# A bidirectional state-space layer with a soft mixture of experts: a PSUM bank held one step longer and one more step before each norm is scaled

## The chip, the cores and the metric

The kernel runs on one core of one Trainium2 chip. The metric is the device time of one execution in microseconds (us); of several executions the median is given. Shorter is better. The five engines of the core run at the same time, each with its own queue: PE (TensorE) multiplies and transposes, DVE (VectorE), ACT (ScalarE) and POOL (GpSimd) work on 128 partitions by so many columns, and SP (SyncE) starts DMAs, as ACT's queue does here as well.

## The reference, cut to what matters

The input is 16 batches of 512 positions by 256 channels, float32. One layer of two parts is computed, each with a residual and a layer norm after it:

```python
xf, res = jnp.split(x @ in_proj_w.T, [512], axis=-1)
xf = silu(causal_dw_conv(xf, conv_w, conv_b))            # 4 taps along the positions
y  = ssm(xf, res, forward weights)
xb = silu(causal_dw_conv(xf, conv_b_w, conv_b_b))        # the backward taps read xf
y  = (y + ssm(xb, res, backward weights, reverse=True)) @ out_proj_w.T
x  = layernorm(x + y)                                    # the "m" norm
x  = layernorm(x + soft_moe(x))                          # the "c" norm
```

`ssm` makes a step size `dt` by a softplus, then for each of 512 channels and 16 states a recurrence along the 512 positions, multiplies it by a factor of its own and sums over the states; `res` gates the sum. The mixture has 16 experts of 64 slots: after a norm, softmax weights gather positions into slots (dispatch), each expert is a gated pair of matrices, and a second softmax brings the slots back to positions (combine).

## The kernel before, in words

`seq_layers` runs over the 16 batches. Each batch has four calls of `scan_part`, for forward and backward (r = 0, 1) and for two pairs of channel chunks (p = 0, 1), in the order (0,0), (1,0), (0,1), (1,1). A call runs over the 16 states in pairs and over two chunks of 128 channels: 16 half-steps. A batch has 64 of them and the kernel 1024.

**A half-step** makes two states of one chunk, each of 128 x 512. POOL multiplies `db` = `du` x `bs` (L403), ACT makes the decay by an exp (L420) and the factor `th` by a tanh (L422), DVE runs the recurrence as a scan (L426 forward, L428 backward) and `hg` = (`th` + 1) x `h` (L431), POOL multiplies `hg` by `cs` (L432), and PE adds `hg` by eight transposing matmuls into the PSUM accumulators `acc` (L347), two half-steps later. `bs` and `cs` come by DMA from SP's queue. For the pairs with the states 5 and 13 (`DIAG`) one state of the pair is made on PE by a diagonal matrix (`hd`, L381). Buffers: `db` 3, `hg` 4, `th` 3, `h` 3 in PSUM.

**Beside the scan** run generators in three lanes, each an object of the class `Side` (L448 to L510). `prep` makes what the next scans need: `prep_forward` (transposes, projection, forward taps), `turn_back` (the backward taps, L223 to L230), `prep_backward` (silu at L235 and the projection `px`), `prep_pair` (`dt`, `rr`, `du`), `prep_gate` and `turn_pair` (`duT`, copied at L331). `front` holds `finish` (transposes of the gated sum at L598, out projection, residual, norm m) and the dispatch; `back` holds the experts and `combine` (norm c). After each half-step `beside_scan` (L517) calls `take_up` of every lane, then begins pieces of work: one of `prep` each time, one of `front` or `back` when its credit has grown to 1.

**What the marks mean.** A generator stops at a `yield`. A positive number tells how many PSUM banks the next piece needs; `HOLD` says that a bank was filled and that what reads it is to be issued at the next `take_up`; `WAIT` is the same without a bank. There are three banks in a ring (`BANKS`, handed out by `bank` at L105). A piece is not begun if the banks handed out since the oldest one held, and those it needs, are more than three (L486 to L488). A half-step that is about to make a state by the diagonal calls `take_up` once more ahead of it (L440, L441), so a lane that stands at a mark is moved twice in that half-step.

**The order of the work** on each engine is made by a scheduler when the program is built; instructions wrapped in `late` keep their place in program order and the others may be moved ahead.

**The norms.** `row_moments` makes means and variances on DVE. `factors` makes from them the scale and shift on POOL, four operations on 128 x 4 (L575 to L578: `m_rs`, `m_sh`, or `c_rs`, `c_sh`); `finish` makes a second factor `r2` by four more (L624 to L627). `scaled` applies them by four ACTIVATEs of ACT (L583). In `finish` one `WAIT` stands between moments and factors and two between factors and `scaled` (after L627), then come the store of x1 on ACT's queue (L631) and `xn` (L635). In `combine` it is the same (`WAIT`s at L955, L957 and L958); there `put` scales and stores the output on ACT's queue (L930). After the last batch a tail (L997 to L1021) finishes batch 15 and runs the experts and combines of the last two batches, with eight banks; there `combine` scales row by row, without those marks.

**The backward taps.** `taps` makes a convolution of one chunk: an ACTIVATE writes the bank `pb` (L171), DVE adds three taps (L177), the last of which writes to `xb` in SBUF. Its first three columns are complete in the bank only, and ACT copies them (L229).

Of the kernel before, what the change touches and what calls it, by code (L numbers as in the profile page):

```python
# [28 lines left out]
KW = 4  # L29
# [10 lines left out]
HOLD, WAIT, GAP = -1, -2, 8  # L40
# [13 lines left out]
def seq_layers(tc, ident, neghalf, a, out):  # L54
# [20 lines left out]
    nc = tc.nc  # L75
    nb = a["x"].shape[0]
    with ExitStack() as ctx:
# [27 lines left out]
        def bank(name):  # L105
            count[0] += 1
            if tail and count[0] % 8 >= 3:
                return tail[0].tile([P, 512], F32, tag="tps", name=name)
            return ps.tile([P, 512], F32, tag="mps", name=name)
# [54 lines left out]
        def late(ins):  # L164

            return tc.keep_in_program_order(ins)

        def taps(dst, src, w, c, last):

            late(  # L170
                nc.scalar.activation(  # L171
                    dst, src, AF.Identity, bias=w["cb"][:, c : c + 1], scale=w["cw"][:, c, KW - 1 : KW]
                )
            )
            for j in range(1, KW):
                o = last if j == KW - 1 else dst
                ins = nc.vector.scalar_tensor_tensor(  # L177
                    o[:, j:], src[:, : L - j], w["cw"][:, c, KW - 1 - j : KW - j], dst[:, j:], ALU.mult, ALU.add
                )
                if j == 1:  # L180
                    late(ins)
# [41 lines left out]
        def turn_back(b, fwd, out):  # L223
            xb = p1.tile([P, ND, L], F32, tag="xb", name=f"xb_{b}")
            for c in range(ND):
                yield 1
                pb = bank(f"pb_{b}_{c}")
                taps(pb, fwd["u"][:, c, :], side[1], c, xb[:, c, :])
                nc.scalar.copy(xb[:, c, 0 : KW - 1], pb[:, 0 : KW - 1])  # L229
            out["u"] = xb  # L230

        def prep_backward(b, out):
# [348 lines left out]
        def scaled(dst, src, sh, rs):  # L581
            for i in range(src.shape[1]):
                ins = nc.scalar.activation(  # L583
                    dst[:, i, :], src[:, i, :], AF.Identity, bias=sh[:, i : i + 1], scale=rs[:, i : i + 1]
                )
                if i == 0:
                    late(ins)

        def finish(b, y):

            xt = load_x(b)
            for h in range(NL // 2):
                yts = []
                for lc in (2 * h, 2 * h + 1):
                    yield 1
                    pt = bank(f"pyt_{b}_{lc}")
                    for c in range(ND):
                        nc.tensor.transpose(  # L598
                            pt[:, c * P : (c + 1) * P], y[:, c, lc * P : (lc + 1) * P], ident
                        )  # L600
                    yield HOLD
                    yt = p2.tile([P, L], F32, tag="fr", name=f"yt_{b}_{lc}")
                    late(nc.scalar.copy(yt, pt))  # L603
                    yts.append(yt)
                yield GAP + 1
                po = bank(f"po_{b}_{h}")
                for i, yt in enumerate(yts):
                    for c in range(ND):
                        nc.tensor.matmul(  # L609
                            po[:, i * DM : (i + 1) * DM],  # L610
                            yt[:, c * P : (c + 1) * P],
                            outT[:, c, :],
                            start=(c == 0),
                            stop=(c == ND - 1),
                        )
                yield HOLD
                x2 = xt[:, 2 * h : 2 * h + 2, :].rearrange("p c d -> p (c d)")
                late(nc.vector.tensor_tensor(x2, x2, po, ALU.add))
            mv = row_moments(nc, p2, xt, "m1")
            yield WAIT  # L620
            rs, sh = factors(mv, "m1")

            r2 = p2.tile([P, NL], F32, tag="m1_r2", name=f"m1_r2_{b}")
            nc.gpsimd.tensor_tensor(r2, mv[:, :, 1], rs, ALU.mult)  # L624
            nc.gpsimd.tensor_tensor(r2, r2, rs, ALU.mult)
            nc.gpsimd.tensor_scalar(r2, r2, EPS, None, ALU.add)
            nc.gpsimd.tensor_tensor(r2, r2, neghalf[:, :NL], ALU.pow)  # L627
            yield WAIT
            yield WAIT
            scaled(xt, xt, sh, rs)  # L630
            nc.scalar.dma_start(x1_dram[b].rearrange("(c p) d -> p c d", p=P), xt)  # L631
            yield 0
            xn = p1.tile([P, NL, DM], F32, tag="xn", name=f"xn_{b}")
            for i in range(NL):
                ins = nc.scalar.activation(xn[:, i, :], xt[:, i, :], AF.Identity, scale=r2[:, i : i + 1])  # L635
                if i == 0:
                    late(ins)
            yield WAIT
            x2T = p1.tile([P, NM, L], F32, tag="x2T", name=f"x2T_{b}")
            for k in range(NM):  # L640
                yield GAP + 1
                pt = bank(f"px2_{b}_{k}")
                for lc in range(NL):
                    nc.tensor.transpose(
                        pt[:, lc * P : (lc + 1) * P], xn[:, lc, k * P : (k + 1) * P], ident
                    )
                yield HOLD
                late(
                    nc.scalar.activation(
                        x2T[:, k, :], pt, AF.Identity, bias=shift[:, k : k + 1], scale=gain[:, k : k + 1]  # L650
                    )
                )
            nc.scalar.dma_start(x2_dram[b].rearrange("k p l -> p k l"), x2T)
            yield from dispatch(b, xn, x2T)
# [249 lines left out]
        def combine(b, kept=None):  # L904

            own = e_dram[:, b * SL : (b + 1) * SL, :].rearrange("(c j) s o -> j s c o", j=2)
            eos = []
            for c0 in range(0, NSC, 4):
                if wide:
                    t = wide[0].tile([P, 4, DM], F32, tag="ceo", name=f"ceo_{b}_{c0}", bufs=4)  # L910
                else:
                    t = p2.tile([P, 4 * DM], F32, tag="W", name=f"ceo_{b}_{c0}", bufs=3)
                    t = t.rearrange("p (c o) -> p c o", c=4)
                for j in range(2):
                    nc.sync.dma_start(t[j * SL : (j + 1) * SL, :, :], own[j][:, c0 : c0 + 4, :])
                eos.append(t)
            if wide and b % 2:
                x1 = p1.tile([P, NL, DM], F32, tag="x", name=f"cx1_{b}")
            else:
                x1 = p1.tile([P, NL, DM], F32, tag="cx1", name=f"cx1_{b}")  # L920
            nc.sync.dma_start(x1, x1_dram[b].rearrange("(c p) d -> p c d", p=P))
            x2 = [] if kept else [load_x2(b, 0)]
            yield 0

            def moments(lo, hi):
                return row_moments(nc, p2, x1[:, lo:hi, :], f"c{hi - lo}"), f"c{hi - lo}"

            def put(lo, hi, rs, sh):
                scaled(x1[:, lo:hi, :], x1[:, lo:hi, :], sh, rs)
                nc.scalar.dma_start(out[b].rearrange("(c p) d -> p c d", p=P)[:, lo:hi, :], x1[:, lo:hi, :])  # L930

            for lc in range(NL):
                i = f"{b}_{lc}"
                cts, sm = kept.pop((b, lc)) if kept else (yield from weights(b, lc, x2, False))
                yield GAP + 1
                po = bank(f"cpo_{i}")
                for sc in range(NSC):
                    nc.tensor.matmul(  # L938
                        po[:, :DM],
                        cts[sc // 4][:, sc % 4 * P : (sc % 4 + 1) * P],  # L940
                        eos[sc // 4][:, sc % 4, :],
                        start=(sc == 0),
                        stop=(sc == NSC - 1),
                    )
                yield HOLD
                late(
                    nc.vector.scalar_tensor_tensor(
                        x1[:, lc, :], po[:, :DM], sm, x1[:, lc, :], ALU.mult, ALU.add
                    )
                )  # L950
                if kept is not None:
                    put(lc, lc + 1, *factors(*moments(lc, lc + 1)))
            if kept is None:
                stats = moments(0, NL)
                yield WAIT  # L955
                both = factors(*stats)
                yield WAIT  # L957
                yield WAIT  # L958
                put(0, NL, *both)

        FINISH, COMBINE, PAIR = 32, 14, 4
# [106 lines left out]
```

## Time and profile before

| | |
|---|---|
| median of 3 runs | 5432.52 us (5432.14 to 5433.58) |
| profiled execution | 5434.84 us |
| its span in the profile | 5432.9 us |
| mean granted TensorE clock | 0.89 |
| PE busy | 4336.3 us (80%) |
| DVE busy | 4552.0 us (84%) |
| ACT busy | 4091.6 us (75%) |
| POOL busy | 4732.3 us (87%) |
| DMA moved | 907.73 MB, mean 167 GB/s |

The profile is of one execution. The span is from the first recorded instruction to the end of the last; the time of the execution is 1.9 us more. A line of a group names line, engine, operation, output and inputs, and gives after the bar the busy time in us, the mean of one in ns, the idle time just before them and what ended most of it. A line of the waits names the waiting instruction, what it waited for, the total in us, the number of times and the longest. A line of a timeline gives start, duration, engine, line and operation, and in brackets the idle time ahead of it and the instruction that ended it. Idle time on an engine that does not bound a stage costs nothing.

Cut by the end of each batch's last product on POOL, the span falls into batches of these lengths:

| stretch | us |
|---|---|
| batch 1 to 2 | about 300 each |
| batch 3 | 320.9 |
| batch 4 | 311.7 |
| batch 5 | 326.9 |
| batches 8, 9, 10 | 311.7, 326.8, 311.6 |
| batch 15 | 369.6 |
| tail | 279.1 |

### The profile page before, as it was taken

To read this page: it belongs to the slowest core of one execution; us is meant where nothing else is said; L and a number is where in the kernel's file an instruction comes from. 1 tells how busy PE (TensorE), PEld (TensorE's weight loads), DVE (VectorE), ACT (ScalarE), POOL (GpSimd) and SP (SyncE) were. 2 spreads that over 40 slices of the span, in tenths; PEclk is the share of its full clock that TensorE was granted. 3 is DMA by queue.
4 is the path that set the end of the run, shared out by engine and by line. 5 is a ranking of instruction groups with operands and counts; after the bars stand their busy time and mean duration, and the time that the engine had idled before them with its cause. 6 is when DMAs were issued, how large, how long until landed. Compare 5 with 4: busy or idle time off the path is not lost. (4 is left out here: it accounts for less than half of the span.)

```text
span 5432.9 us, 73685 instructions
## 1 busy us (share of the span) xinstructions
PE 4336.3 (80%) x24145; PEld 3393.4 (62%) x24145; DVE 4552.0 (84%) x6276; ACT 4091.6 (75%) x6517; POOL 4732.3 (87%) x2537
## 2 busy tenths in 40 slices
PE   4656666898878977788788978889777887878889
PEld 3545555676667765677656766667656775667657
DVE  6888989889888898888988988988989889887722
ACT  6677777887788777887878887788778887777641
POOL 6999999999999899998999989998999989988600
PEclk7677878898889989899889988899888998989999
DMA  4333434575446754566446754467444774457435
GB/s 129 130 122 132 130 124 131 192 231 161 151 141 212 228 148 145 157 220 213 134 137 195 230 173 150 130 215 231 151 145 143 226 224 132 144 178 234 126 104 184
DMA packets 595237, 907.73 MB, mean 167 GB/s; under 512 B 78083, under 2 KB 384899, under 8 KB 594853
## 3 DMA queue, kind: packets, MB, share of 16 engines
q1 hardware_dynamic: 521156, 859.87, 49.9%
q10 hardware_dynamic: 73696, 43.14, 2.8%
q8 instruction: 192, 3.15, 0.2%
q14 instruction: 193, 1.57, 0.1%
HBM read 840.86 MB, written 62.01 MB: 166 GB/s over the span
## 5 line engine op out<-in xcount | busy, mean ns | idle before, releaser
L432 POOL TENSOR_TENSOR hg<-hg,cs 128x1024 f32<-128x1024 f32 x1024 | 2415.3, 2362 | 129.7 <-DVE hg L431 111.4
L403 POOL TENSOR_TENSOR db<-du,bs 128x1024 f32<-128x1024 f32 (+1 forms) x1024 | 2138.8, 2092 | 240.4 <-DVE h L426 93.5
L347 PE MATMUL acc<-ident,hg 128*128 128x128 f32 x8192 | 1191.7, 296 | 207.3 <-POOL hg L432 183.2
L431 DVE SCALAR_TENSOR_TENSOR hg<-th,h 128x512 f32<-128x512 f32 x1792 | 1186.2, 678 | 188.8 <-PE acc L347 110.4
L347 PEld LDWEIGHTS acc<-ident,hg 128*128 128x128 f32 x8192 | 1053.5, 155 | 399.4 <-POOL hg L432 251.0
L426 DVE TENSOR_TENSOR_SCAN h<-h,db 128x512 f32<-128x512 f32 x896 | 1071.3, 1218 | 97.5 <-ACT h L420 92.0
L428 DVE TENSOR_TENSOR_SCAN h<-h,db 128x512 f32<-128x512 f32 x896 | 1072.1, 1218 | 96.1 <-ACT h L420 92.9
L422 ACT ACTIVATE th<-rr,Ah_f 128x512 f32<-128x512 f32 x1024 | 724.5, 714 | 189.2 <-DVE hg L431 187.7
L422 ACT ACTIVATE th<-rr,Ah_b 128x512 f32<-128x512 f32 x1024 | 721.6, 712 | 166.1 <-DVE hg L431 151.3
L420 ACT ACTIVATE h<-dt,A_f 128x512 f32<-128x512 f32 x896 | 608.0, 681 | 115.2 <-DVE hg L431 112.1
L420 ACT ACTIVATE h<-dt,A_b 128x512 f32<-128x512 f32 x896 | 608.6, 681 | 105.0 <-DVE hg L431 102.9
L663 PE MATMUL pl<-x2T,seT 128*128 128x512 f32 x512 | 286.0, 687 | 73.6 <-DVE hg L431 36.2
L381 PE MATMUL hd<-dg,duT 128*128 128x128 f32 x2048 | 309.0, 300 | 35.3 <-ACT yt L603 15.2
L806 PEld LDWEIGHTS pg<-st,Wg 128*128 128x128 f32 x2048 | 245.4, 196 | 107.8 <-issue 85.4
L381 PEld LDWEIGHTS hd<-dg,duT 128*128 128x128 f32 x2048 | 286.1, 216 | 41.8 <-ACT yt L603 17.8
L938 PE MATMUL cpo<-ceo,ct 128*128 128x256 f32 x1024 | 266.3, 420 | 48.5 <-DVE rr L313 38.8
L782 PE MATMUL peo<-Wd,ht 128*128 128x256 f32 x1024 | 253.5, 403 | 48.2 <-DVE rr L313 30.5
L755 PE MATMUL pu<-st,Wu 128*128 128x128 f32 x2048 | 252.3, 282 | 44.6 <-DMA Wu<-in_Wu_dram 18.6
L755 PEld LDWEIGHTS pu<-st,Wu 128*128 128x128 f32 x2048 | 242.6, 196 | 55.8 <-DVE h L428 17.6
L938 PEld LDWEIGHTS cpo<-ceo,ct 128*128 128x128 f32 x1024 | 214.0, 213 | 99.6 <-DVE rr L313 44.0
L806 PE MATMUL pg<-st,Wg 128*128 128x128 f32 x2048 | 270.3, 287 | 5.6 <-DMA Wg<-in_Wg_dram 3.6
L860 PE MATMUL cl<-seT,cx 128*128 128x512 f32 x512 | 251.3, 631 | 29.1 <-ACT et L674 18.2
(151 smaller groups left out, 6621.3 us busy)
## 6 DMA issues: line engine op xcount, KB each, us to landing
cs<-bc SPq DMA_DIRECT2D x512, 512.0 KB, 4.0
bs<-bc SPq DMA_DIRECT2D x384, 512.0 KB, 5.0
Wg<-in_Wg_dram SPq DMA_DIRECT2D x128, 512.0 KB, 6.1
Wu<-in_Wu_dram SPq DMA_DIRECT2D x128, 512.0 KB, 5.7
Wd<-in_Wd_dram SPq DMA_DIRECT2D x128, 512.0 KB, 5.5
dg<-diag_dram SPq DMA_DIRECT2D x128, 256.0 KB, 4.4
bs<-bc SPq DMA_DIRECT2D x128, 256.0 KB, 3.6
x<-in_x_dram SPq DMA_DIRECT2D x32, 512.0 KB, 6.6
```

What stands on the lines that cost most here:

```text
L347: ins = nc.tensor.matmul(accs[c][:, s], hc[:, j, s], ident, is_transpose=True, start=False, stop=(last and j == 1 and lc == NL - 1),)
L381: ins = nc.tensor.matmul(h[:, s], v[c][3][:, s], dg[:, s], start=True, stop=True)
L403: nc.gpsimd.tensor_tensor(db[:, :k, :], du.unsqueeze(1).to_broadcast([P, k, L]), bs[:, :k, :], ALU.mult)
L420: nc.scalar.activation(hs[j][1], dt, AF.Exp, scale=w["A"][:, c, s])
L422: nc.scalar.activation(ths[j], rr, AF.Tanh, bias=LN_1E12 / 2, scale=w["Ah"][:, c, s])
L426: nc.vector.tensor_tensor_scan(h, dec, add, 0.0, ALU.mult, ALU.add)
L428: nc.vector.tensor_tensor_scan(h[:, ::-1], dec[:, ::-1], add[:, ::-1], 0.0, ALU.mult, ALU.add)
L431: nc.vector.scalar_tensor_tensor(hg[:, j, :], th, 1.0, h, ALU.add, ALU.mult)
L432: nc.gpsimd.tensor_tensor(hg, hg, cs, ALU.mult)
L755: nc.tensor.matmul(pu[:, fc * P : (fc + 1) * P], got["Wu", e][:, k, fc * P : (fc + 1) * P], st[:, k, :, j * SL : (j + 1) * SL], start=(k = ...
L806: nc.tensor.matmul(pg[:, fc * P : (fc + 1) * P], got["Wg", e][:, k, fc * P : (fc + 1) * P], st[:, k, :, j * SL : (j + 1) * SL], start=Fals ...
L938: nc.tensor.matmul(po[:, :DM], cts[sc // 4][:, sc % 4 * P : (sc % 4 + 1) * P], eos[sc // 4][:, sc % 4, :], start=(sc == 0), stop=(sc == NS ...
```

## The change

Three lines are added and one is wrapped. In `turn_back` the bank of the backward taps is held (`yield HOLD`) until the next `take_up`, and the copy of its three columns is issued then and kept in program order. In `finish` and in `combine` a third `WAIT` stands between the making of the factors and the scaling.

```diff
@@ turn_back
                 pb = bank(f"pb_{b}_{c}")
                 taps(pb, fwd["u"][:, c, :], side[1], c, xb[:, c, :])
-                nc.scalar.copy(xb[:, c, 0 : KW - 1], pb[:, 0 : KW - 1])
+                yield HOLD
+                late(nc.scalar.copy(xb[:, c, 0 : KW - 1], pb[:, 0 : KW - 1]))
             out["u"] = xb
@@ finish
             nc.gpsimd.tensor_tensor(r2, r2, neghalf[:, :NL], ALU.pow)
+            yield WAIT
             yield WAIT
             yield WAIT
             scaled(xt, xt, sh, rs)
@@ combine
                 both = factors(*stats)
                 yield WAIT
                 yield WAIT
+                yield WAIT
                 put(0, NL, *both)
```

## The prediction, made before the changed kernel was run

> **What bounds the kernel now.** I read the busy table first, then the batches as windows, then the waits, then the timelines of the places that the edit touches. Busy times (us, share of the span, instructions) and the two costliest groups:
>
> ```profile
> PE 4336.3 (80%) x24145; PEld 3393.4 (62%) x24145; DVE 4552.0 (84%) x6276; ACT 4091.6 (75%) x6517; POOL 4732.3 (87%) x2537
> L432 POOL TENSOR_TENSOR hg<-hg,cs 128x1024 f32<-128x1024 f32 x1024 | 2415.3, 2362 | 129.7 <-DVE hg L431 111.4
> L403 POOL TENSOR_TENSOR db<-du,bs 128x1024 f32<-128x1024 f32 (+1 forms) x1024 | 2138.8, 2092 | 240.4 <-DVE h L426 93.5
> ```
>
> POOL is the fullest engine, and these two lines are nearly all of it. Windows cut where a batch's last POOL product ends (batches 8, 9, 15 and the tail; the columns after the length are PE, PEld, DVE, ACT, POOL busy, clock, DMA share, GB/s):
>
> ```profile
> 2557.80:2869.50 311.70, 248.31 (x1281) 187.55 (x1279) 283.42 (x387) 247.36 (x414) 295.11 (x158) 0.87 0.44 138
> 2869.50:3196.30 326.80, 284.13 (x1740) 231.17 (x1739) 283.21 (x395) 263.90 (x400) 295.33 (x157) 0.94 0.67 214
> 4784.20:5153.80 369.60, 310.72 (x1838) 249.08 (x1838) 284.22 (x414) 265.24 (x416) 287.85 (x152) 0.94 0.59 188
> 5153.80:5432.90 279.10, 249.73 (x1246) 185.91 (x1244) 67.94 (x191) 77.30 (x153) 14.68 (x44) 0.96 0.45 141
> ```
>
> POOL has 295 us of work in either kind of batch; an even one idles it 16.6 us, an odd one 31.5 us. The edit adds no POOL instruction, so inside batches 1 to 14 it can only buy or lose POOL gaps: about 6 x (16.6 + 31.5) = 289 us over the six even (4 to 14) and six odd ones (3 to 13) that carry both kinds of norm. Batch 15 idles it 82 us, where PE has 311 us of work; the tail has almost no POOL work.
>
> The waits that the edit is aimed at (total us, times, longest):
>
> ```profile
> ACT cx L583 <- POOL c_sh L578: 96.9, 22, 20.8
> PE pyt L598 <- ACT xb L229: 60.1, 13, 6.3
> ACT x L583 <- POOL m_sh L578: 44.3, 11, 8.6
> POOL hg L432 <- DVE hg L431: 111.4, 60, 7.5
> ```
>
> They sum to 201 us on ACT and PE, but neither is the bound. What reaches POOL is seen place by place. Start of batch 8, PE and then POOL; c norm of batch 8, ACT, DVE, POOL; m norm of batch 9, ACT, PE, DVE, POOL (start, duration, idle before and its releaser):
>
> ```profile
> 2572.28 1.11 PE L598 MATMUL pyt<-ident,res 128*128 128x128 f32 x4 [3.62 <-ACT xb L229]
> 2572.73 4.69 POOL L403 TENSOR_TENSOR db<-du,bs 128x1024 f32<-128x1024 f32 x2 [3.16 <-issue]
> 2741.55 1.58 ACT L583 ACTIVATE cx<-cx,c_sh,c_rs 128x256 f32<-128x256 f32 x3 [4.16 <-POOL c_sh L578]
> 2745.26 1.23 DVE L426 TENSOR_TENSOR_SCAN h<-h,db 128x512 f32<-128x512 f32 x1 [5.64 <-ACT h L420]
> 2748.53 2.34 POOL L403 TENSOR_TENSOR db<-du,bs 128x1024 f32<-128x1024 f32 x1 [2.39 <-DVE h L426]
> 2959.43 0.60 ACT L583 ACTIVATE x<-x,m_sh,m_rs 128x256 f32<-128x256 f32 x1 [3.99 <-POOL m_sh L578]
> 2960.55 3.04 PE L191 MATMUL pres<-w_pres,xT 128*128 128x128 f32 x16 [3.86 <-ACT duT L331]
> 2967.74 0.69 DVE L843 TENSOR_TENSOR eo<-peo,bd 128x512 f32<-128x512 f32 x1 [3.14 <-PE peo L782]
> 2971.61 2.37 POOL L403 TENSOR_TENSOR db<-du,bs 128x1024 f32<-128x1024 f32 x1 [3.53 <-DVE h L428]
> ```
>
> The reader is to see a relay: ACT stands at L583 for factors that POOL has not made; exps behind it are late; DVE has no scan; POOL then waits for that scan to free `db`. A 4 us wait on ACT becomes 2.4 to 3.5 us on POOL. At the start of a batch it is otherwise: in the timeline of VectorE between 2555 and 2582 us there is no idle time (a burst of taps at L177 fills it), so POOL's 3.16 us is DVE's work, and PE's 3.62 us behind the copy costs nothing.
>
> **What the Trainium skill says.** "Perfetto Trace Analysis", Tensor Engine Instruction: ACT, DVE and GpSimd are strict FIFO. The trace agrees: exps and tanhs behind the waiting L583 start only after it. "ScalarE: Activation LUTs", What ACT_TABLE_LOAD costs: 1283 ns a load, whatever the set, plus a drain; the rows of L420 show loads of 1283 ns, 121 of them. "GPSIMD Engine Reference", 1. Specifications: GpSimd shares its SBUF interfaces with VectorE when that reads two SBUF inputs; in this trace POOL's L432 is 2362 ns on average and 2350 to 2400 in busy and idle stretches alike, so I price no contention.
>
> **The change part by part.** What stands before what in the changed kernel I read from the order of its instructions on each engine, set beside that of the kernel before. No engine gets more arithmetic.
>
> *The held bank.* L229 (64 copies, 152 ns) leaves the turn of its taps and comes a half-step (about 4.6 us, two POOL products) later, in program order on ACT. Of the three banks one is held longer, and no piece is begun whose banks would pass three counted from the oldest held (L486), so the backward taps, projections and pairs, with the weight loads on SP's queue that belong to them, come one half-step later. They were issued a half-step or more ahead of use, so I cost the loads at nothing; uncovered, a half-step per batch, 4.6 us. Fewer taps then stand in the burst of a batch's start (two before the third scan where there were three). One tap is 0.66 us of DVE: the gap of 3.16 becomes 2.5. Six even batches: gain 6 x 0.65 = **3.9 us**. Bounds 0 (the tap was hidden) to 6 x 3.16 = 19 (burst broken up). Removing PE's 60 us of waits is costed at nothing: DVE's burst covers it. With that cover gone it would be worth up to 13 x 3.6 = 47 us.
>
> *The added WAIT on the m norm.* One half-step is meant, but a half-step that makes a state by the diagonal takes up WAITs twice (L440), so in the order most m norms still stand two half-steps behind their factors. What changes in odd batches is that both `duT` copies (L331) go ahead of L583. Then PE's `pres` no longer waits 3.86, nor `eo` 3.14. ACT's wait falls by the two copies' 1.05, to about 2.8, and DVE's exposed part nearly goes. Of POOL's 3.53 I count 2.8 gained (bounds 0 and 3.5): 6 x 2.8 = **16.8 us**. Behind L583 on ACT stand the x1 store (L631) and `xn`; both come later, and the dispatch, due a batch later, hides that. If it did not, PE would lose one half-step per batch, 16 x 4.6 = 74 us at most.
>
> *The added WAIT on the c norm, even batches.* Here it is eaten and more: the factors move too, behind another pair of `db`, and the distance falls from two half-steps to one. ACT then waits up to 8 us (its 4.16 plus a product and a half), and POOL's next `db` comes 1.3 us later: a loss of 6 x 1.3 = **7.8 us** (bounds: 0, and 4.0 each if all of the extra wait arrives). After it POOL's gaps of 2.89 and 0.57 at 2760 us lose about 1 us, since the scan is then already late and no longer meets `cnm`: gain **6.0 us** (bounds 0 and 3.5 each).
>
> *The c norm at the start of odd batches.* L583 and its store (L930) now stand ahead of the third backward tap group, and POOL makes the factors one `db` (2.36) later. ACT waits 3 to 6 us in place of 4.11 (2891.79), DVE behind it 2.9 to 5.6, POOL 1.1 to 3.9 more. I take 2.5: a loss of **15.0 us** over six batches (bounds 1.1 and 3.9).
>
> *Second half of odd batches.* With prep later by a half-step, the taps of the next batch and `ht` (L767) no longer stand in one burst; the two POOL gaps of that burst (2.99 and 2.38 at 3084 to 3090) shrink by about 1.4, and in the order a `db` now stands between two `hg` where POOL waited 5.17 at 3142.91. That fills at most 2.36; I take 0.8. Gain 6 x 2.2 = **13.2 us** (bounds 0 and 5.4 + 2.4 each).
>
> *Table loads.* The order has 324 where there were 342: two fewer in each odd batch but the last, six fewer there. In the loop ACT is not the bound (264 of 327 us busy), so nothing. In batch 15 it stands on the path part of the time: 6 x 1.283 = 7.7 us, half of it, **4 us** (bounds 0 and 7.7).
>
> *Tail.* One more WAIT in the last `finish`; combine there has none. 0, bounds -3 and +3. SP's and POOL's queues keep their order there.
>
> Sum: 3.9 + 16.8 - 7.8 + 6.0 - 15.0 + 13.2 + 4.0 = 21.1 us. The profiled execution took 5434.8 us (2 us around its span of 5432.9); less 21.1 is 5413.7. It lies 2.3 us above the median of 5432.5, so the median becomes **5411 us**, 0.4% faster.
>
> **The rivals.** *(A) Full gain:* all norm waits leave ACT and with them the POOL gaps: even c 2.39 + 2.89, odd start 3.96, odd m 3.53: 6 x 12.8 = 77 us, to 5356. For it: the relays above. Against: the order hardly shows the third step. *(B) It doesn't do what it says:* WAITs eaten, gaps only shift, gains and losses within 10 us: 5430. For it: the distances. Against: `duT` does move. *(C) Slower:* L583 of the odd start, now ahead of the taps on a strict queue, and the one-step distance in even batches stop ACT for up to 8 us while DVE has about one scan and gate (1.8 us) in stock; from the point where the factors land more than that late, each further us arrives at POOL. Priced at the upper bounds: 6 x (4.0 + 3.9) = 47 us lost, less 16.8 + 3.9 + 4.0 = 25 gained: 5455. For it: the 4.16 already gives DVE 5.64. Against: POOL, when late, makes later waits shorter.
>
> **How the numbers follow.** Forecast (5385 to 5421) 0.50; A 0.10; B 0.22; C 0.18. A measurement of this kernel tells about 0.2%, 10.9 us, from no change. The forecast and A are all faster, B lies in the band but for 0.01, C (5444 to 5465) is all slower: faster 0.61, same 0.21, slower 0.18. The range runs from 5378, leaving out most of A, to 5452, leaving out over half of C: about 0.18 outside.
>
> **What would show it.** Right: the m wait down to about 30 us in total, no `eo` wait of 3 us after it, odd batches near 324 us, even ones near 311, 324 table loads, POOL busy unchanged at 295. PE's wait on L229 gone with no even-start gap below 2.4. Wrong: the c waits below 60 us in total with POOL's gaps after them gone (A); odd batches longer than 328 us with a gap over 6 us after the first c norm (C); POOL's own products longer, or the tail changed by over 5 us, which no step above has.

## The result, and the profile after

The changed kernel takes 5481.1 us (median of 4 runs, 5477.2 to 5484.4) against 5432.3 us before: 1.0091 of before, 95% interval 1.0076 to 1.0106. It is 0.9% slower; 0.4% faster was forecast, and the time lies above the range given.

The page of the changed kernel, busy time by engine. Every line of code after L229 stands one to three lines lower (L583 is L584 there):

```profile
PE 4354.9 (79%) x24141; PEld 3430.5 (63%) x24145; DVE 4550.4 (83%) x6276; ACT 4070.3 (74%) x6499; POOL 4732.7 (86%) x2537
```

POOL's work is what it was (4732.7 against 4732.3 us), DVE's too, and ACT lost 18 table loads (6517 to 6499 instructions, as forecast). So the loss is waiting. The windows of batches 8, 9, 15 and of the tail, cut as before:

```profile
2565.70:2880.70 315.00, 239.33 (x1271) 182.05 (x1270) 282.23 (x386) 247.18 (x413) 294.96 (x157) 0.91 0.44 137
2880.70:3214.30 333.60, 292.13 (x1748) 238.56 (x1747) 283.70 (x396) 261.88 (x400) 295.54 (x158) 0.92 0.65 210
4826.10:5198.90 372.80, 314.61 (x1838) 252.18 (x1839) 283.65 (x413) 257.12 (x409) 288.15 (x152) 0.93 0.58 186
5198.90:5482.40 283.50, 253.74 (x1256) 189.06 (x1255) 68.00 (x193) 78.73 (x157) 14.69 (x44) 0.95 0.44 139
```

The lengths rise by 3.3, 6.8, 3.2 and 4.3 us, with POOL's busy column unmoved. Cut so, the whole span of 5482.4 us differs from that of before by 49.5: batch 0 +1.6, batches 1 and 2 -8.3, batch 3 +0.7, the six even batches 4 to 14 +14.4, the five odd ones 5 to 13 +33.6, batch 15 +3.2, tail +4.3. (The tail is between 273.9 and 283.5 us in the profiles of all the kernels below, so its 4 us are not laid to the edit.)

The waits that the edit is aimed at:

```profile
ACT cx L584 <- POOL c_sh L579: 111.3, 22, 21.0
ACT x L584 <- POOL m_sh L579: 70.6, 15, 10.2
PE pyt L599 <- ACT xb L230: 49.2, 9, 9.3
ACT xb L230 <- DVE xb L177: 50.0, 34, 3.9
ACT et L676 <- DVE nm L670: 132.2, 82, 4.5
```

They were 96.9, 44.3 and 60.1 us in the first three, so both waits for norm factors grew, although each scaling has a step more. (Of the first, 42 us before and 46 us after lie in the tail, which has no such step.) The fourth was 14.1 us: the copy that was held now makes ACT wait for its taps. The fifth, the dispatch's exp behind the maximum of its logits, was 102.8 us.

To find the places (one execution of each kernel), take the end of each of POOL's 64 products `hg` of a batch (L432 or L433 in the timeline), count from the batch's start, and subtract the same of the kernel before. For batch 9, an odd one, at half-steps counted from 0 (us later than before):

| kernel | 7 | 15 | 21 | 31 | 47 | 53 | 63 |
|---|---|---|---|---|---|---|---|
| changed | 5.7 | 6.5 | 1.9 | 1.9 | 3.6 | 6.0 | 6.8 |
| held bank alone | 5.7 | 4.4 | 2.0 | 1.6 | 3.0 | 3.0 | 3.0 |
| norm m's WAIT alone | 2.6 | 0.3 | -1.0 | 1.1 | 1.3 | 3.6 | 4.4 |
| norm c's WAIT alone | 2.7 | 2.8 | 3.7 | 3.7 | 3.7 | 3.7 | 3.7 |
| held bank, norm m | 5.7 | 4.4 | -0.1 | -0.3 | 4.8 | 9.7 | 10.1 |
| held bank, four in order | 2.5 | 2.0 | -2.5 | -2.5 | -2.5 | -2.5 | -2.5 |

Batch 9 is an example, not a mean: the odd batches 5 to 13 of the changed kernel end 8.5, 4.2, 6.8, 7.2 and 6.9 us late, those with held bank and norm m 10.7, 1.2, 10.1, 3.8 and 3.9.

Three things happen to batch 9: it loses near 6 us in its first eight half-steps, gains about 4 at norm m (from 15 to 21), and loses again in its second half. The first loss, in the timelines of ACT, DVE and POOL in batch 9 of the changed kernel:

```profile
2899.31 0.16 ACT L230 COPY xb<-pb 128x3 f32<-128x3 f32 x1 [3.90 <-DVE xb L177]
2904.17 0.60 ACT L584 ACTIVATE cx<-cx,c_sh,c_rs 128x256 f32<-128x256 f32 x1 [4.70 <-POOL c_sh L579]
2904.68 0.76 ACT L171 ACTIVATE pb<-xf,cb_b,cw_b 128x512 f32<-128x512 f32 x1
...
2905.99 1.57 ACT L584 ACTIVATE cx<-cx,c_sh,c_rs 128x256 f32<-128x256 f32 x3
...
2905.47 0.76 DVE L177 SCALAR_TENSOR_TENSOR pb<-xf,cw_b,pb 128x511 f32<-128x511 f32 x1 [4.60 <-ACT pb L171]
...
2908.72 2.37 POOL L433 TENSOR_TENSOR hg<-hg,cs 128x1024 f32<-128x1024 f32 x1 [4.58 <-issue]
2913.24 2.36 POOL L404 TENSOR_TENSOR db<-du,bs 128x1024 f32<-128x1024 f32 x1 [2.15 <-DVE h L427]
```

One of the four ACTIVATEs of the c norm stands alone ahead of the third group of backward taps (L171), and the other three behind. ACT waits 4.70 us for the factors at that one, DVE waits 4.60 for the taps behind it, and POOL, which has two products `db` in hand and no `hg`, 4.58 and 2.15. The same place in the kernel before, ACT and POOL:

```profile
2891.79 2.08 ACT L583 ACTIVATE cx<-cx,c_sh,c_rs 128x256 f32<-128x256 f32 x4 [4.11 <-POOL c_sh L578]
2893.77 0.76 ACT L171 ACTIVATE pb<-xf,cb_b,cw_b 128x512 f32<-128x512 f32 x1
...
2891.72 2.35 POOL L432 TENSOR_TENSOR hg<-hg,cs 128x1024 f32<-128x1024 f32 x1
```

There ACT waits for the same factors, 4.11 us. But three groups of taps have already passed ACT and only the fourth stands behind the norm, DVE has scans and products `hg` left to do and waits 0.67 us, and POOL does not wait at all. Why one ACTIVATE stands alone in the changed kernel is what the experiments found.

### The profile page after: what moved, and what is told of

It is laid out like the page before. It is cut to its first block, busy times and chain, and to the rows that moved or that the text cites. A ratio compares the mean times of both kernels' runs of the same rounds, so it can differ in the third digit from the quotient of the medians.

```text
span 5482.4 us, 73584 instructions
## 1 busy us (share of the span) xinstructions
PE 4354.9 (79%) x24141; PEld 3430.5 (63%) x24145; DVE 4550.4 (83%) x6276; ACT 4070.3 (74%) x6499; POOL 4732.7 (86%) x2537
## 3 DMA queue, kind: packets, MB, share of 16 engines
q14 instruction: 192, 1.56, 0.1%
## 5 line engine op out<-in xcount | busy, mean ns | idle before, releaser
L433 POOL TENSOR_TENSOR hg<-hg,cs 128x1024 f32<-128x1024 f32 x1024 | 2419.5, 2365 | 188.1 <-DVE hg L432 99.9
L348 PE MATMUL acc<-ident,hg 128*128 128x128 f32 x8192 | 1206.6, 299 | 210.6 <-POOL hg L433 179.0
L348 PEld LDWEIGHTS acc<-ident,hg 128*128 128x128 f32 x8192 | 1070.1, 156 | 415.9 <-POOL hg L433 237.5
L432 DVE SCALAR_TENSOR_TENSOR hg<-th,h 128x512 f32<-128x512 f32 x1792 | 1183.8, 678 | 168.6 <-PE acc L348 110.1
L421 ACT ACTIVATE h<-dt,A_f 128x512 f32<-128x512 f32 x896 | 610.2, 682 | 125.8 <-DVE hg L432 123.6
L697 PE MATMUL pq<-dis,xn 128*128 128x256 f32 x1024 | 252.4, 403 | 18.3 <-DVE rr L314 13.2
```

The source lines that it names most:

```text
L348: ins = nc.tensor.matmul(accs[c][:, s], hc[:, j, s], ident, is_transpose=True, start=False, stop=(last and j == 1 and lc == NL - 1),)
L421: nc.scalar.activation(hs[j][1], dt, AF.Exp, scale=w["A"][:, c, s])
L432: nc.vector.scalar_tensor_tensor(hg[:, j, :], th, 1.0, h, ALU.add, ALU.mult)
L433: nc.gpsimd.tensor_tensor(hg, hg, cs, ALU.mult)
```

## The experiments: which edit does it

Each run changes the kernel before unless told otherwise. The ratios are to the kernel before on the same chip, where it took 5434.7 to 5437.0 us, with 95% intervals.

**The held bank alone** (the diff of `turn_back` only).

> Only the held bank of the backward taps; both norms as before. Theory N (the loss comes from the third WAIT of norm c, which puts its scaling ahead of the third and fourth group of backward taps): within 8 us of before (5424 to 5440), and no POOL gap above 4 us in the first eight half-steps of an odd batch. Theory H (the copy, now in program order, stops ACT's queue for the last tap, 3.9 us in the changed kernel, and the exps behind it): +25 to +45 us, most of it in those eight half-steps. Theory I (the loss needs both edits together): within 8 us here and in the run of norm c alone.

Measured: 5434.2 us, 0.9999 (0.9990 to 1.0007). The total fits theories N and I, but the place does not fit N: at half-step 7 of batch 9 it is 5.7 us late, just as the changed kernel, with a POOL gap of 4.59 us where N allowed 4. Gains elsewhere (batch 15 alone is 3.7 us shorter) make up for it. In the order of instructions it makes no difference whether the copy is wrapped in `late`, and wrapping it without holding the bank gives the order of before; it is the later step, not the kept place, that moves things.

**The third WAIT of norm m alone.**

> Only the third WAIT of norm m. All theories take the gain in the changed kernel at the m norm (4 us in batches 1 and 2, 3.6 us in odd batches) to be this edit's: 5432 less 2 x 4 and 6 x 3.6 = 5402, range 5396 to 5412. If the gain belongs to the held bank instead, this run stands at 5432 and that of the held bank alone is about 30 us faster.

Measured: 5446.9 us, 1.0025 (1.0016 to 1.0034), slower, where a gain of about 0.5% was expected. The gain at norm m is there (3.4 us in batches 1 and 2, 1.3 in batch 9 from half-step 15 to 21), but odd batches give it back and more in the second half: the row of the table goes from -1.0 to 4.4.

**The third WAIT of norm c alone.**

> Only the third WAIT of norm c. Theory N: +35 to +70 us, with a POOL gap of 4 to 5 us in the first eight half-steps of odd batches. Theory H: within 15 us. Theory I: within 8 us.

Measured: 5429.1 us, 0.9988 (0.9981 to 0.9995). Theory N is wrong: this edit gains a little, which theories H and I allow. Even batch 8 is 4.3 us shorter, odd batch 9 3.7 us longer.

**The changed kernel without that WAIT** (held bank and norm m).

> The changed kernel without the third WAIT of norm c. Theory N: faster than before by about the m norm's 30 us, 5395 to 5415. Theory H: 5430 to 5450. Theory I: 5395 to 5415.

Measured: 5482.7 us, 1.0089 (1.0074 to 1.0104): the whole loss, without norm c's WAIT. N is out, and so is I, which had expected a gain here; H does not give it either, since the held bank alone costs nothing in sum. Held bank and norm m's WAIT together cost 0.9%, though alone they cost 0.0 and 0.25%.

## The experiments: the second half of odd batches

What norm m's WAIT moves besides the norm is everything behind it in the front lane. In the order on PE the dispatch's first logits come at half-step 25 of the batches 3 to 14 in place of 23. In batch 9 of the changed kernel that is 141.9 us after the batch's start, against 123.6 before.

**A WAIT behind the scaling**, so that the norm stays and only what follows it is later:

```diff
             nc.scalar.dma_start(x1_dram[b].rearrange("(c p) d -> p c d", p=P), xt)
+            yield WAIT
             yield 0
```

> The kernel before with one more WAIT behind the scaling of norm m and the store, ahead of xn: the norm is scaled where it was, and the rest of the front lane (dispatch) begins its logits at the same half-steps as in the run with the third WAIT of norm m alone (25 in place of 23). Theory P (the phase of the dispatch costs the time): no gain at half-step 18 of batches 1 and 2, a loss of 3 to 6 us in the second half of odd batches as in that run, +20 to +40 us in all. Theory S (the scaling's own later place costs it): within 5 us of before.

Measured: 5460.5 us, 1.0053 (1.0038 to 1.0068), 4.2 us late at the end of batch 9, all of it gathered in the second half (0.2 at half-step 31). Batches 1 and 2 gain about a microsecond or two, where P had expected nothing and norm m's WAIT gives 3.4. So the phase of the dispatch, the half-step at which it begins, costs time without any change to a norm.

**The third WAIT with the phase kept**: the WAIT between norm m's moments and its factors is taken out.

```diff
             mv = row_moments(nc, p2, xt, "m1")
-            yield WAIT
             rs, sh = factors(mv, "m1")
...
+            yield WAIT
             yield WAIT
             yield WAIT
             scaled(xt, xt, sh, rs)
```

> The third WAIT of norm m, with the WAIT between its moments and factors taken out: the factors come a half-step earlier, the scaling and the dispatch begin where they did before (half-step 23). Theory P: the losses of the second half of odd batches are gone (below 1 us), and norm m gains 1 to 3.6 us in batches 1, 2 and odd ones: 5405 to 5425. Theory S: as the run of norm m's WAIT alone, 5440 to 5450. POOL may wait for moments that now come just ahead of the factors; that would show at half-step 18 as a loss.

Measured: 5414.4 us, 0.9964 (0.9951 to 0.9977). Batch 9 keeps its gain at norm m (-4.5 us at half-step 21) and loses 1.1 us of it in the second half, slightly more than P allowed. Theory P holds in both directions, but batches 1 and 2 gain nothing here, where it had expected 1 to 3.6 us.

The profiles of all the kernels say the same. Take POOL's idle time from half-step 39 to 63 in each of the odd batches 5 to 13. In the five kernels whose dispatch begins there at half-step 25 it is 17.5 to 22.2 us; in the twelve where it begins at 23, the kernel before among them, 15.1 to 17.2.

What meets what is seen in the second half of batch 9 of the changed kernel, DVE and then POOL:

```profile
3150.35 0.72 DVE L177 SCALAR_TENSOR_TENSOR xf<-pin,cw_f,xf 128x509 f32<-128x509 f32 x1
3150.99 0.68 DVE L670 TENSOR_REDUCE nm<-pl 128x1 f32<-128x512 f32 x1
3151.59 0.68 DVE L432 SCALAR_TENSOR_TENSOR hg<-th,hd 128x512 f32<-128x512 f32 x1
...
3153.32 0.15 DVE L677 RECIPROCAL sm<-sm 128x1 f32<-128x1 f32 x1
...
3154.49 2.29 DVE L177 SCALAR_TENSOR_TENSOR xf<-pin,cw_f,xf 128x511 f32<-128x511 f32 x3
...
3159.27 0.69 DVE L432 SCALAR_TENSOR_TENSOR hg<-th,hd 128x512 f32<-128x512 f32 x1
...
3152.40 2.35 POOL L433 TENSOR_TENSOR hg<-hg,cs 128x1024 f32<-128x1024 f32 x1 [2.53 <-issue]
...
3160.10 4.69 POOL L433 TENSOR_TENSOR hg<-hg,cs 128x1024 f32<-128x1024 f32 x2 [3.00 <-DMA bs<-bc]
3166.89 2.36 POOL L404 TENSOR_TENSOR db<-du,bs 128x1024 f32<-128x1024 f32 x1 [2.10 <-issue]
```

and POOL at this place in the kernel before:

```profile
3135.37 2.37 POOL L432 TENSOR_TENSOR hg<-hg,cs 128x1024 f32<-128x1024 f32 x1 [0.67 <-issue]
3142.91 2.36 POOL L432 TENSOR_TENSOR hg<-hg,cs 128x1024 f32<-128x1024 f32 x1 [5.17 <-DVE hg L431]
```

The next batch's taps (L177) stand on DVE, and the dispatch's maximum (L670) and reciprocal (L677) now fall among them. POOL waits 7.6 us in three gaps where the kernel before had 0.67 and 5.17. The first two end 0.13 and 0.14 us after DVE's `hg` (L432), so DVE sets them; the second is put down to the DMA of `bs`, which that product does not read. How the third comes about, and what each instruction of the dispatch adds, is open.

**WAITs only where no experts run** (norm c's for all, norm m's for batches 0 and 1 only).

> The third WAIT of norm c for all batches and that of norm m for the first two only, where no experts run beside it; no held bank. Theory P: the run of norm c's WAIT alone less 2 x 3.4 us: 5418 to 5426, with all batches from 3 on as in that run. Theory S expects the same, since both give batches 1 and 2 the gain.

Measured: 5428.1 us, 0.9983 (0.9975 to 0.9992), 2 us above the expected range. Batches 1 and 2 gain 2.3 and 4.4 us, but batches from 3 on are not quite those of norm c alone (batch 8 -0.8 against -4.3): a different order early on moved later ones. It tells nothing apart.

## The experiments: the start of odd batches

**The held bank with four WAITs in norm c**, to bring its scaling behind the taps.

> The held bank and four WAITs in norm c in place of two; norm m as before. In the order of ACT the scaling of norm c then stands behind the fourth group of backward taps instead of ahead of the third, while POOL's order around the factors is that of the run with the held bank alone. Theory Q (what costs 5.7 us in the first eight half-steps of an odd batch is ACT's queue standing at the scaling ahead of the third group of taps): there 2 us or less in place of 5.7. Theory R (it is POOL's two products ahead of the factors, or the taps' being a half-step later): 5 to 6 us remain. Total: Q 5400 to 5415, R 5425 to 5445.

Measured: 5419.4 us, 0.9969 (0.9962 to 0.9976), and at half-step 7 of batch 9 7.1 us late. By its expectation theory Q is out; but the premise failed. ACT in batch 9 of this kernel:

```profile
2889.85 0.60 ACT L584 ACTIVATE cx<-cx,c_sh,c_rs 128x256 f32<-128x256 f32 x1 [4.69 <-POOL c_sh L579]
2890.36 0.76 ACT L171 ACTIVATE pb<-xf,cb_b,cw_b 128x512 f32<-128x512 f32 x1
```

With two WAITs (held bank alone, at 2895.31), three (changed kernel) or four, one ACTIVATE of the norm is ahead of these taps. The reason is in `scaled`: only the first of its four ACTIVATEs is kept in program order, and the scheduler moves others ahead. The WAITs move the first one alone. In batch 8 this can be seen: three ACTIVATEs go first and the kept one follows, 2.4 us after their start in the kernel before (2741.55 and 2743.98), 4.8 us in the changed one (2744.48 and 2749.32).

**All four in program order**, with the held bank; norms with the WAITs of before.

```diff
                 ins = nc.scalar.activation(
                     dst[:, i, :], src[:, i, :], AF.Identity, bias=sh[:, i : i + 1], scale=rs[:, i : i + 1]
                 )
-                if i == 0:
-                    late(ins)
+                late(ins)
```

> The held bank alone, and in the scaling of a norm all four ACTIVATEs are kept in program order; before, and in all runs so far, only the first of the four was, and the others could be moved ahead. In the order of ACT none of the four now stands ahead of the third group of backward taps (in the run with four WAITs one or more still did). The taps stay a half-step later and POOL still has two products ahead of the factors. Theory Q: at half-step 4 of batch 9 2 us or less in place of 5.8. Theory R: 5 to 6 us remain. Total: Q 5405 to 5425, R 5428 to 5440.

Measured: 5369.9 us, 0.9880 (0.9865 to 0.9894). ACT and POOL at the same place, and then ACT at the c norm of batch 8, here and in the changed kernel:

```profile
2861.61 0.76 ACT L171 ACTIVATE pb<-xf,cb_b,cw_b 128x512 f32<-128x512 f32 x1
...
2866.85 2.08 ACT L584 ACTIVATE cx<-cx,c_sh,c_rs 128x256 f32<-128x256 f32 x4
2868.84 0.77 ACT L171 ACTIVATE pb<-xf,cb_b,cw_b 128x512 f32<-128x512 f32 x1
...
2868.11 2.35 POOL L433 TENSOR_TENSOR hg<-hg,cs 128x1024 f32<-128x1024 f32 x1 [1.56 <-DVE hg L432]
```

```profile
2712.25 2.08 ACT L584 ACTIVATE cx<-cx,c_sh,c_rs 128x256 f32<-128x256 f32 x4 [0.58 <-POOL c_sh L579]
...
2744.48 1.58 ACT L584 ACTIVATE cx<-cx,c_sh,c_rs 128x256 f32<-128x256 f32 x3 [6.77 <-POOL c_sh L579]
```

The third group of taps (2861.61) is now ahead of the norm. The four ACTIVATEs run together and wait for nothing; POOL's 4.58 and 2.15 have become 1.56 and, 10 us later, 1.08. Batch 9 is 2.1 us late at half-step 4 and 2.5 at half-step 7, against 5.8 and 5.7 with the held bank alone. Q had said 2 or less at half-step 4, R 5 to 6. The held taps and the two `db` ahead of the factors are still there, so theory R falls and Q stands, but for some 2 us that are left until norm m. In batch 8 the wait is 0.58 us where it was 4.16 before and 6.77 in the changed kernel, and the even batch is 303.7 us long in place of 311.7. The total is far below what Q had allowed, since its numbers left the even batches out: these give 50 us.

**The changed kernel with all four in order.**

> The changed kernel with all four ACTIVATEs of a scaling kept in program order. Theory Q: the 5.8 us at half-step 4 of odd batches go, 4 to 6 us in each of six, so 5445 to 5460; what remains above before is the dispatch's phase. Theory R: 5472 to 5487.

Measured: 5411.1 us, 0.9953 (0.9938 to 0.9968): 70 us below the changed kernel, more than Q had expected, for the same reason. ACT's wait for `m_sh` is now 3.2 us in total, against 70.6: with the order kept the third WAIT does what it says. But batch 9 ends 8.7 us late against before, all of it from the second half (-0.1 at half-step 31), where the dispatch has its late phase. Batches 7, 11 and 13 end 5.8 to 8.9 us late; batch 5, with the same phase, gains 1.2, so the phase does not cost the same everywhere.

**All four in order, nothing else.**

> The kernel before with all four ACTIVATEs of a scaling kept in program order, nothing else. If keeping the order gains only where the held bank has moved the taps behind the norm: 0.996 to 1.003 of before. If it gains by itself: 0.985 to 0.992, as with the held bank.

Measured: 5404.7 us, 0.9934 (0.9917 to 0.9950). This lies between the two ranges: it gains by itself, about half as much as with the held bank. Batch 8 is 3.8 us shorter and batch 9 3.4; there the gain comes at norm m, whose ACTIVATEs are kept in order too, and the first 16 half-steps are unchanged. Batch 0, which scales the slot embeddings by the same function, is 5.5 us longer. The held bank, worth nothing alone, adds about 0.5% to it, in the second half of even batches: from half-step 39 to 63 POOL idles 3.0 to 3.9 us in each of them with both, and 5.4 to 10.0 in all other kernels.

Set side by side, the edit costs 0.9% where only the first ACTIVATE is kept in order (1 to 1.0091) and 0.2% where all four are (0.9934 to 0.9953, with intervals that overlap).

**The changed kernel with both repairs**: all four in order, and the WAIT ahead of norm m's factors taken out.

> The changed kernel with both repairs: all four ACTIVATEs in order, and the WAIT ahead of norm m's factors taken out so that the dispatch of odd batches begins at half-step 23 again. If the phase is what is left: the loss of 8 us in the second half of batch 9 is below 2 us, and the time 5411 less about 6 x 8 = 5365, range 5355 to 5380. If not: 5400 to 5415.

Measured: 5369.8 us, 0.9877 (0.9862 to 0.9891). Batch 9 stays at -1.7 us from half-step 31 to 63. The two repairs together remove the loss and 63 us more. They overlap with what the kernel before had already: the order alone gains there too. The changed kernel with the phase alone repaired was not run, so the loss is not split between the two.

**The same with two WAITs in norm c.**

> As the run before it, with two WAITs in norm c. If the third one matters once the order is kept: 3 to 10 us away from the run before it, either way. If not: the same within 3 us.

Measured: 5369.1 us, 0.9876 (0.9861 to 0.9890): no different. Once the order is kept, and the phase, neither added WAIT can be seen in the time: the held bank with four in order, without them, has 0.9880.

**Without the held bank**, the WAIT of norm c and that of norm m with the phase kept.

> No held bank; the third WAIT of norm c, and that of norm m with the WAIT ahead of its factors taken out, so that the dispatch keeps its phase. If the two gains add (0.9964 and 0.9988 of before): 0.995 of before, about 5409. If the WAIT of norm c gives back in odd batches what it gains in even ones: 0.996 to 0.997.

Measured: 5410.9 us, 0.9955 (0.9940 to 0.9970), between the two expectations.

**The same with all four in order.**

> As the run before it, with all four ACTIVATEs of a scaling kept in program order. If ACTIVATEs moved ahead of their place are what makes ACT stand in the c norms of odd batches too: 2 to 4 us less in each of six, 5390 to 5400. If not, as the run before it, 5405 to 5412.

Measured: 5419.6 us, 0.9974 (0.9967 to 0.9981), outside both. Keeping the order, worth 0.66% by itself, is worth nothing beside these two WAITs without the held bank. Why was not followed up; the parts do not add, and each run has its own order.

## Why the prediction was wrong, step by step

*The bound* was right: POOL's busy time did not move, and the loss in batches 1 to 14 is POOL idle time. (L432 was read as 2350 to 2400 ns in all stretches; single ones run from 2327 to 2431.)

*The c norm at the start of odd batches* failed by size: a loss of 2.5 us was taken, 3.9 the most; 5.7 was measured in batch 9. The mechanism was named there and as rival C (the scaling ahead of the third group of taps on a strict queue), and the trace agrees with the Trainium skill's strict FIFO ("Perfetto Trace Analysis", Tensor Engine Instruction): the taps' ACTIVATE starts only behind the one that waits, and DVE's 4.60 us is ACT's 4.70 passed on. But the prediction put the whole scaling and its store ahead of these taps, where one ACTIVATE of four stands, and it did not say which edit does it. The held bank does it alone: the third group of taps, a half-step later, now stands behind an ACTIVATE that the scheduler moves ahead. Norm c's WAIT, which theory N blamed, makes the kernel 0.1% faster when alone. Its six odd batches were taken as 3 to 13; batch 3 has no c norm at its start, and batches 5 to 15 have one.

*The second half of odd batches* failed in sign: 2.2 us gained was forecast, 4.9 lost measured (1.9 at half-step 31, 6.8 at 63). The sentence that failed is that the x1 store and `xn` come later "and the dispatch, due a batch later, hides that". That the dispatch itself starts two half-steps later is not hidden, as the runs with its phase moved alone and put back show (+0.5%, and -0.4% with norm m's step kept). Of the gaps that were to shrink, 2.99 and 2.38 became 0.60, 1.52 and 2.69, and the one of 5.17 did not shrink but became part of the 7.6 us above. This step and the last are about 5 x (5.7 - 2.5) + 5 x (4.9 + 2.2) = 52 us of the 70 us between forecast and result, with batch 9 taken for all five.

*Norm m* was right for POOL and wrong for ACT: 2.8 us in odd batches were forecast, about 4.5 measured from half-step 15 to 21 of batch 9, 3.6 of them from half-step 18 to 19. The `duT` copies do go ahead, and POOL's gap of 3.53 us is gone. But ACT's wait there was to fall to 2.8 us, and rose from 3.99 to 5.97:

```profile
2969.07 1.11 ACT L332 COPY duT<-pdu 128x512 f32<-128x512 f32 x2
2976.14 1.09 ACT L584 ACTIVATE x<-x,m_sh,m_rs 128x256 f32<-128x256 f32 x2 [5.97 <-POOL m_sh L579]
...
2977.67 1.28 POOL L404 TENSOR_TENSOR db<-du,bs 128x512 f32<-128x512 f32 x1
2978.92 2.35 POOL L433 TENSOR_TENSOR hg<-hg,cs 128x1024 f32<-128x1024 f32 x1
```

So a wait on ACT does not become a gap on POOL by a fixed share, as the relay of the prediction has it. Here 5.97 us cost POOL nothing, and neither did 4.11 us at the c norm of batch 9 before the change, while 4.70 us there after it cost 4.58. The three places differ in what stands behind the wait and in what DVE and POOL still have in hand. The 4 us in each of batches 1 and 2 were missed.

*Even batches*: 0.65 gained at the start was forecast and 0.2 measured; the c norm and what follows it were forecast at a loss of 0.3 net. Batch 8 in fact ends 3.4 us late, 2.0 of it at half-step 21, where only held bank and norm m together show it. No step had that.

*Batch 15* was forecast to gain 4 us from six fewer table loads and lost 3.2. The loads did go (18 in all). Nothing shows that they were on the path.

*The rivals*: A could not come, since the waits never left. What the prediction held against A, that the order hardly shows the third step, was seen but not asked after: for norm m the reason was one `if` in `scaled`, since with the order kept its wait all but goes (3.2 us). C had the direction and the start of odd batches. Its price of 5455 us left out the second half, and its sign, a gap of over 6 us after the first c norm, did not come (4.58 us).

## What to carry to other kernels

A step that is given to a group of instructions delays only those that are held to their place. Where a scheduler may move the rest, look at where each of them lands, and fix the group as a whole before its distance is tuned.

A wait added in a lane also delays all that follows in that lane. Try the delay by itself, behind the thing it was meant for, and give it back elsewhere in the lane; if the time moves with the phase, the phase was the cost.

Parts of such a change do not add: here 0.0%, +0.25% and -0.12% alone made +0.9% together.

## What the runs showed that was not expected

Nothing new of the hardware: a whole `db` took 2.37 us, a table load 1283 ns and four ACTIVATEs of a scaling in a row 2.08 us in the orders looked at. What surprised is how exactly a schedule repeats. The kernel with norm c's WAIT alone has the order of the kernel before up to batch 4, and the lengths of its batches 1 to 3 differ by 0.3 us at most. So a step of half a microsecond at one half-step of a batch can be read from one profile each. Batch 0, at the start, differs by 1.5 us all the same, and whole executions of the kernel before lay up to 20 us apart on one chip, so this does not hold for totals.
